# Four seams of a four-layer kernel: where a table is built, rows are returned, and a scan is opened

## The chip, the cores and the metric

One Trainium2 chip, one of its cores, one launch. The time is device microseconds of that core (us below); a kernel is timed in several runs and the median is given. The engines named here are PE (TensorE matmul; PEld is its weight load), DVE (VectorE), ACT (ScalarE), POOL (GpSimd) and SP (SyncE, which only issues transfers).

## The reference

Two images of 128 channels and 56 x 56 pixels go through four layers, each added onto x after a group norm: agent attention, a 3 x 3 convolution, a mixture of experts on 2 x 2 patches, and a selective scan in two directions along each row. The change touches the last two:

```python
# layer 2: 1568 patches (784 an image) of 512 numbers, 8 experts, two for each patch
logits = xp @ router_w
probs = softmax(logits)
topv, topi = top_k(probs, 2);  topv = topv / topv.sum(-1, keepdims=True)
gate = (one_hot(topi, 8) * topv[..., None]).sum(1)
for e in range(8):
    val, g = split(xp @ w1[e], 2, axis=-1)
    out = out + gate[:, e:e+1] * ((val * sigmoid(g)) @ w2[e])

# layer 3, once forwards and once backwards along each row of 56 pixels
xi, z = split(x @ in_w.T, 2)
xc = silu(conv_b + sum(xp[:, k:k+L] * conv_w[:, k] for k in range(4)))
dt, B, C = split(xc @ xproj_w.T, [8, 24])
dt = softplus(dt @ dt_w.T + dt_b)
h = exp(dt * A) * h + (dt * xc) * B        # 16 states for each channel
y = (h * C).sum(states) + xc * D
out = (y * silu(z)) @ out_w.T
# both directions are fused, layer-normed and added onto x
```

## The kernel before

**Experts, the table.** `PatchExperts.route` routes the patches and lays them, sorted by image and expert, into 32 tiles of 128 slots. Patches lie in 14 groups of 112 (T), seven an image. For each group and each of the two choices, `is_slot` (112 x 128) says which slot of its tile a patch takes, and `what` (112 x 64) which tile, once times the patch's number and once times its share. Lines 1291 to 1299 multiply `is_slot` transposed by `what` and sum 28 products into the bank `inv` (128 slots x 64), from which `whom` (the patch of each slot, L1301) and `share` are copied. `is_slot` and `what` lie in `room0` and `room1`, which share buffers with the expert weights (tags w2 and w1).

**Experts, the tiles.** `run` takes tile after tile. SP reads the expert's number and issues the loads of its weights (`up_weights` 4 MB, L1331; `down_weights` 2 MB, L1336), two buffers of each. `gather` fetches the 128 patches of a tile from DRAM by `whom`, an indirect transfer that POOL issues (L1306), four buffers. `up` transposes the rows (`xr_ps`, L1354), copies them (`xs_c`, L1356) and makes two halves (c) of two parts each, 16 products to a part (`h_ps`, L1365; in float32 a product is two passes), then sigmoid on ACT (L1375) and the product on DVE (`ht`, L1377). `down` (L1385, 16 passes of 512 columns) follows one tile later; ACT scales the result and stores it in `os` (L1388, L1389). 25 tiles are always there (`fewest`); the first image's are all within the first 20 (`ahead`). The rest (three here) stand in a Switch over their number.

**The return.** `combine` brings the results back into x: for each group of 112 patches two gathers from `os` (g0, g1; L1306), an add on DVE (L1461), four transposes on PE (`y_ps`, L1464), and, one call later, `onto`: four adds onto x (L1437) and their statistics (L88). It is a generator; one `next` traces one group. `arrive` runs it and then the three stages of the group norm (aggregate; means, one small product, L104; deviations, another, L116, then Ln and Exp on ACT, L67 and L68). The first image's runs beside the tiles: three leading calls (`LEAD`) at tile 20 that issue gathers only, and from then on a call at each `spot`: after either half of `up` and after `down`. The second image's runs in the opening of layer 3, without a lead.

**Layer 3.** `mamba_pair` works on 14 blocks of 448 pixels and two ways (f, b). A way has 16 units. A unit is a decay (`dA`, ACT, two instructions, L1876), a `push` (`dBu`, POOL, L1887), a `scan` (DVE, L1906), and the product with C on DVE (L1917) or POOL (L1915; `POOLED` says which), which PE then sums (`collect`, L1928). Ahead of a way's units stand its stages: `norm`, `conv` (L1752), `silu`, `low` (L1781), `step` (L1806), `log`, `softplus` (L1841), `weigh` (L1849), `send_steps` (SP and POOL transfers, L1864). They are booked by step in `agenda`. Under `manual_schedule` each engine takes the instructions of a block in the order in which they are traced. There are two such blocks: the opening (all steps below zero, and with them the second image's return), and the units' loop, which starts with `push` of the first four units, and then, at unit n, traces the decay of n + 1, what the last step left to fetch, the push of n + 4, the scan of n, a collect, and the steps booked for n. PSUM has one bank each under the tags mm and c, and two double banks under dA.

Of the kernel before, what the change touches and what calls it, by code (L numbers as in the profile page):

```python
# [8 lines left out]
F32 = mybir.dt.float32  # L9
# [8 lines left out]
P = 128  # L18
# [3 lines left out]
BLK = 448  # L22
# [991 lines left out]
class PatchExperts:  # L1014
# [15 lines left out]
    def route(self, dram, wpool, conv):  # L1030
# [9 lines left out]
        with tc.tile_pool(name="l2_route", bufs=1) as one, tc.tile_pool(  # L1040
# [13 lines left out]
            nc.vector.tensor_reduce(four, net.ident.rearrange("p (q e) -> p e q", q=4), AX.X, ALU.add)  # L1054
            shape = [T, nt, experts]
# [194 lines left out]
            inv = ps.tile([P, 512], F32, name="inv", tag="tr")  # L1250
# [4 lines left out]
            for n, room in enumerate(rooms):  # L1255
# [27 lines left out]
                for some in (range(per), range(per, nt)):  # L1283
# [7 lines left out]
                    for t in some:  # L1291
                        nc.tensor.matmul(
                            inv[:, : 2 * TILES],
                            is_slot[:, t, :],
                            what[:, t].rearrange("t h j -> t (h j)"),
                            start=n == 0 and t == 0,
                            stop=n == 1 and t == nt - 1,
                        )

            self.whom = keep.tile([P, TILES], I32, name="whom")  # L1300
# [14 lines left out]
    def run(self, wpool, work, ps, beside):  # L1315
# [12 lines left out]

        def up_weights(j, e):
            w1 = ups[j % 2]  # L1330
            nc.sync.dma_start(w1, w1s[e].rearrange("o c q f -> (o c) q f"))  # L1331
            return w1
# [8 lines left out]
        def spot():  # L1341
            with net.tc.issue_after(traced[0]):
                next(beside, None)
# [6 lines left out]
        def up(j, w1, xr):  # L1350
# [7 lines left out]
            for c in range(2):  # L1358
                parts = []
                for part in (1, 0):  # L1360
# [11 lines left out]
                    traced[0] = mm.ins  # L1372
                    parts.append(h_ps)
                sg = work.tile([P, 4 * SLOTS], F32, name="sg", tag="sg")
# [3 lines left out]
                if self.ahead + 1 < j + c < self.fewest + c:  # L1378
                    spot()
# [14 lines left out]
        for j in range(self.fewest):  # L1394
            e = expert(j)
            w1, w2 = up_weights(j, e), down_weights(j, e)
            ht = up(j, w1, gather(j))
            if last is not None:
                down(*last)
            last = (j, ht, w2)  # L1400
            if j == self.ahead:
                for _ in range(LEAD):
                    next(beside)
            elif j > self.ahead:
                spot()
# [77 lines left out]
LEAD = 3  # L1483
# [96 lines left out]
def arrive(net, combine, b, gathered, bank, banks, pool, norms, lead=0):  # L1580
# [3 lines left out]
    for stage in net.norm_stages(b, banks, "mm", got.append):  # L1584
        fetch = stage()
        if fetch:
            fetch()
        yield
# [7 lines left out]
def mamba_pair(net, out, wts, combine, keep, norms):  # L1596
# [19 lines left out]
    with ExitStack() as ctx:  # L1616
# [17 lines left out]

        class Banks:
            def tile(self, shape, dtype, name, tag):
                return wide_bank(name)[:, :512]
# [101 lines left out]
        class Half:  # L1739
# [6 lines left out]
            def conv(self, m):  # L1746
# [12 lines left out]
                if m == 0:  # L1759
                    self.xc = work.tile([P, 2, BLK], F32, name="xc", tag=f"xc{w.d}", bufs=1 if w.d == "f" else 2)  # L1760
                return lambda: nc.scalar.activation(
                    self.xc[:, m, :], pm[:, :BLK], AF.Identity, bias=w.conv_b[:, m : m + 1]
                )
# [188 lines left out]
        for n, blk in enumerate(blocks):  # L1952
# [3 lines left out]
            if n == 0:  # L1956

                book(at + 1, blk.norm)
                book(at + 3, lambda f=f: f.conv(0))
                book(at + 4, lambda f=f: f.conv(1), tag="c")  # L1960
                book(at + 6, lambda f=f: silu(f, None))
# [11 lines left out]
                book(at + 17, lambda b=b: b.conv(0))  # L1973
                book(at + 17, lambda b=b: b.conv(1), tag="c")
                book(at + 19, lambda b=b: silu(b, None))
# [67 lines left out]
        with tc.manual_schedule(engines={E.PE, E.Activation, E.DVE, E.Pool, E.SP}):  # L2043
            nc.scalar.preload_act_table_set(EXP_LN)
            second = arrive(net, combine, 1, gathered, wide_bank, ps_of_norms, keep, norms)
            first = min(agenda)
            for step in range(first, 0):
                run(step)
                for _ in range((0, 0, 0, 2, 0, 1, 1, 0, 1, 1, 1, 1, 0, 1, 1, 1)[step - first] if step - first < 16 else 1):
                    next(second, None)  # L2050
                fetch(step + 1)
            for _ in second:
                pass
        with tc.manual_schedule(engines={E.PE, E.Activation, E.DVE, E.Pool, E.SP}):
# [5 lines left out]
            for n, (h, u) in enumerate(units):  # L2060
# [15 lines left out]
                waiting.append((h, u))  # L2076

# [126 lines left out]
```

## Time and profile before

| what | us |
|---|---|
| median of 3 runs | 3035.01 (3030.69 to 3038.34) |
| profiled execution | 3033.16 |
| its span | 3031.1 |
| attention, convolution, routing | 0 to about 1012 |
| slot table, first gathers | 1012 to 1036 |
| expert tiles, both images | 1036 to 1677 |
| opening of layer 3 up to the first scan | 1677 to 1718 |
| units' loop and end | 1718 to 3031 |

The page gives the whole span's busy shares: PE 89%, DVE 72%, ACT 61%, POOL 48%. They are averages over stages with different limits, and each stage is to be read on its own: which engine has no idle time there, and what ended the idle time of the others. In a row of the order of time, the first number is the start, the second how long the group took from first start to last end, and the bracket is the engine's idle time before it and what ended that.

### The profile page before, as it was taken

Reading aid. Unit: us, or ns where it says so; the run is one execution under the profiler, and the core shown is the slowest. Engines: PE = TensorE matmul, PEld = TensorE weight load, DVE = VectorE, ACT = ScalarE, POOL = GpSimd, SP = SyncE. Lnnn points to the kernel's source line nnn. Section 1 sums busy time; section 2 is a strip of 40 time slices with the busy share of each in tenths; the row PEclk is TensorE's granted clock in tenths of the full one; section 3 lists DMA queues with packets and bytes.
Section 4 is the critical chain, followed back from the end, with each engine's and each line's share of the span. In section 5 each row is a group of like instructions: output and inputs, shape, how many; then the busy total and the mean of one; then the engine's idle time right before and its main releaser. Section 6 shows DMA issues by size and latency. Waiting matters only on the chain. (4 is left out here: it accounts for less than half of the span.)

```text
span 3031.1 us, 39355 instructions
## 1 busy us (share of the span) xinstructions
PE 2697.4 (89%) x14924; PEld 1283.4 (42%) x14924; DVE 2184.0 (72%) x1854; ACT 1853.7 (61%) x2944; POOL 1450.5 (48%) x801
## 2 busy tenths in 40 slices
PE   7999999999998799999898778888888888888874
PEld 3333333333335688788777323333333333233321
DVE  5978998999886301010120589999999999999996
ACT  5778788778751100000001488888888888888884
POOL 3000010010322100000100589999999999999995
PEclk9999999999999799999999799899899999999987
DMA  1000000000002668788875554465555565545460
GB/s 55 1 1 1 1 1 1 1 1 1 1 1 60 263 272 318 314 310 321 303 279 206 129 125 116 114 148 130 120 118 121 117 147 127 127 116 120 115 148 22
DMA packets 157934, 369.32 MB, mean 122 GB/s; under 512 B 25156, under 2 KB 114980, under 8 KB 154132
## 3 DMA queue, kind: packets, MB, share of 16 engines
q1 hardware_dynamic: 135744, 339.30, 37.5%
q0 software_dynamic: 5520, 15.62, 1.6%
q10 hardware_dynamic: 16452, 11.61, 1.2%
q8 instruction: 122, 2.00, 0.3%
q14 instruction: 96, 0.79, 0.1%
HBM read 297.89 MB, written 17.20 MB: 104 GB/s over the span
## 5 line engine op out<-in xcount | busy, mean ns | idle before, releaser
L1887 POOL TENSOR_TENSOR dBu<-dtu,Bs 128x896 f32<-128x896 f32 x448 | 921.3, 2094 | 14.4 <-DMA dtu<-sp_u 10.5
L1906 DVE TENSOR_TENSOR_SCAN h<-dA,dBu 128x896 f32<-128x896 f32 x448 | 882.3, 2009 | 28.2 <-ACT dA L1876 24.8
L620 ACT ACTIVATE ex<-sc 128x896 f32<-128x896 f32 (+1 forms) x700 | 602.6, 918 | 124.7 <-PE sc L617 113.4
L1928 PE MATMUL y<-h,both 128*64 128x448 f32 x1792 | 468.2, 615 | 82.2 <-POOL h L1915 74.9
L627 DVE TENSOR_TENSOR ex_sum<-ex_sum,ex 128x1792 f32<-128x1792 f32 (+1 forms) x238 | 492.6, 2070 | 35.3 <-ACT ex L620 21.3
L1365 PEld LDWEIGHTS h_ps<-xs_c,w 128*128 128x128 f32 x3584 | 406.5, 193 | 28.6 <-ACT ot L1388 15.4
L1365 PE MATMUL h_ps<-xs_c,w 128*128 128x128 f32 x3584 | 409.9, 277 | 9.0 <-issue 9.0
L617 PE MATMUL sc<-q,k 32*128 32x448 f32 (+1 forms) x2800 | 403.6, 587 | 3.6 <-ACT ex L620 2.9
L1917 DVE TENSOR_TENSOR h<-h,c_ps 128x1792 f32<-128x1792 f32 (+1 forms) x168 | 326.6, 1944 | 26.9 <-ACT c_ps L1894 10.1
L635 PE MATMUL av<-ex,va 128*32 128x448 f32 (+1 forms) x2800 | 334.3, 552 | 0.1
L582 POOL TENSOR_TENSOR a_e<-a_e,a_inv 112x784 f32<-112x784 f32 x14 | 41.6, 2973 | 584.0 <-ACT ex L620 394.5
L1377 DVE TENSOR_TENSOR ht<-h_ps,sg 128x512 f32<-128x512 f32 x56 | 38.5, 691 | 391.8 <-PE h_ps L1365 339.7
L1876 ACT ACTIVATE dA<-dt,f_A 128x448 f32<-128x448 f32 x448 | 282.7, 636 | 50.7 <-DVE h L1906 39.7
L1876 ACT ACTIVATE dA<-dt,b_A 128x448 f32<-128x448 f32 x448 | 282.8, 635 | 33.1 <-DVE h L1906 24.2
L1928 PEld LDWEIGHTS y<-h,both 128*64 128x64 f32 x1792 | 118.9, 147 | 354.8 <-issue 212.6
L1306 POOL DMA_INDIRECT xr<-xd,whom x28 | 28.1, 1004 | 493.3 <-PE xr_ps L1354 449.3
L1915 POOL TENSOR_TENSOR h<-h,Cs 128x1792 f32<-128x1792 f32 (+1 forms) x70 | 252.5, 3608 | 6.9 <-PE sp_ps L1841 3.4
L617 PEld LDWEIGHTS sc<-q,k 32*128 32x128 f32 (+1 forms) x2800 | 137.7, 181 | 230.1 <-issue 132.5
L1375 ACT ACTIVATE sg<-h_ps 128x512 f32<-128x512 f32 x56 | 33.4, 597 | 310.0 <-PE h_ps L1365 309.9
L1385 PE MATMUL o_ps<-w,ht 128*128 128x512 f32 x448 | 204.4, 601 | 1.2 <-DVE ht L1377 1.2
L1388 ACT ACTIVATE ot<-o_ps,share 128x512 f32<-128x512 f32 x28 | 19.2, 687 | 255.5 <-PE o_ps L1385 255.5
L625 DVE TENSOR_TENSOR ex_sum<-ex 128x1792 f32<-128x1792 f32 x56 | 114.4, 2043 | 54.5 <-ACT ex L620 54.4
(342 smaller groups left out, 3006.7 us busy)
## 6 DMA issues: line engine op xcount, KB each, us to landing
w<-in_L_conv_w_dram SPq DMA_DIRECT2D x28, 4096.0 KB, 20.4
w<-in_L_conv_w_dram SPq DMA_DIRECT2D x28, 2048.0 KB, 10.9
Bs<-far SPq DMA_DIRECT2D x56, 896.0 KB, 7.7
Cs<-far SPq DMA_DIRECT2D x448, 112.0 KB, 2.9
dtu<-sp_u SPq DMA_DIRECT2D x108, 224.0 KB, 3.8
dt<-dt SPq DMA_DIRECT2D x108, 224.0 KB, 4.9
os<-ot ACTq DMA_DIRECT2D x28, 256.0 KB, 7.9
xd<-xt SPq DMA_DIRECT2D x14, 224.0 KB, 2.7
```

The costliest lines, as they stand in the source:

```text
L617: nc.tensor.matmul(sc[:size, j, :BLK], self.m.k[rows, at : at + size], self.q[rows, :], start=True, stop=True)
L620: nc.scalar.activation(ex[:size, 2 * g : 2 * g + 2, :], sc[:size, :, :BLK], AF.Exp, scale=scale)
L627: nc.vector.tensor_add(self.total[g][:size], self.total[g][:size], ex[:size])
L635: nc.tensor.matmul(self.av[rows, :BLK], self.m.va[:size, i, rows], self.ex[i][:size, h, :], start=i == 0, stop=i == STEPS - 1,)
L1365: mm = nc.tensor.matmul(h_ps[:, i * SLOTS : (i + 1) * SLOTS], w1[:, q, f0 : f0 + P], xc[:, q, :], start=q == 0, stop=q == 3,)
L1385: mm = nc.tensor.matmul(o_ps, ht[:, i, :], w2[:, i, :], start=i == 0, stop=i == nj - 1)
L1876: nc.scalar.activation(self.dA[u][:, r * BLK : (r + 1) * BLK], self.dt2[:, m, r, :], AF.Exp, scale=self.w.A[:, j, 2 * m + r : 2 * m + r + 1],)
L1887: nc.gpsimd.tensor_tensor(self.dBu[u], self.dtu2[:, m], self.B[:, j, :].unsqueeze(1).to_broadcast(shape), ALU.mult)
L1906: nc.vector.tensor_tensor_scan(hf, af, bf, 0.0, ALU.mult, ALU.add)
L1915: nc.gpsimd.tensor_tensor(h4, h4, self.C[j].unsqueeze(1).to_broadcast(shape), ALU.mult)
L1917: nc.vector.tensor_tensor(h4, h4, self.c_ps[:, :BLK].unsqueeze(1).to_broadcast(shape), ALU.mult)
L1928: nc.tensor.matmul(self.y[r * H : (r + 1) * H, m, :BLK], both, self.hc[j][:, m, r, :], start=False, stop=j == PAIRS - 1)
```

## The change

Four parts:

- **Slot table by halves.** The operands of the 28 products change places: `what` is loaded, `is_slot` streams, and even and odd groups write to the lower and the upper 64 partitions of a new bank `turned`. It is copied to SBUF (`table`) and multiplied once by `fold` (two stacked identities of 64), which turns it and adds the halves: `inv` as before.
- **Tiles.** PE's work of tiles 1 to 3 is queued behind the first group of tile 0's products; SP's loads of a tile are queued behind the load of up weights of tile 0 (for tile 1) or 1 (later ones).
- **Return of the first image.** Four leading calls and five buffers instead of three and four. The later calls stand at places listed in `turns`: for tile 21 after the `down` that follows it; for tile 22 after the first, third and fourth part of `up` and after `down`; for tile 23 after the second and fourth part and twice after `down`; for tile 24 after the first two parts. At its norm's second stage ACT's table set for Exp and Ln is loaded.
- **Opening of layer 3.** Block 0's two ways apply silu when they read the convolution from its bank, with no second pass. Five of the second image's seven groups are returned in the opening (one after `conv`, one after `low`, one after each of the next three stages), into the dA banks; the other two, the last `onto` and the norm's stages follow in the units' loop, one call a unit right after the scan, into the bank mm.

```diff
@@ route
+            fold = one.tile([P, 2 * TILES], F32, name="fold")
+            nc.vector.tensor_add(fold, net.ident[:, : P // 2], net.ident[:, P // 2 :])
...
-            inv = ps.tile([P, 512], F32, name="inv", tag="tr")
+            turned = ps.tile([P, 512], F32, name="turned", tag="tr")
...
                     for t in some:
+                        g = t % 2 * 2 * TILES
                         nc.tensor.matmul(
-                            inv[:, : 2 * TILES],
+                            turned[g : g + 2 * TILES, :SLOTS],
+                            what[:, t].rearrange("t h j -> t (h j)"),
                             is_slot[:, t, :],
-                            what[:, t].rearrange("t h j -> t (h j)"),
-                            start=n == 0 and t == 0,
-                            stop=n == 1 and t == nt - 1,
+                            start=n == 0 and t < 2,
+                            stop=n == 1 and t >= nt - 2,
                         )
+            table = one.tile([P, SLOTS], F32, name="table")
+            nc.vector.tensor_copy(table, turned[:, :SLOTS])
+            inv = ps.tile([P, 512], F32, name="inv", tag="tr")
+            nc.tensor.matmul(inv[:, : 2 * TILES], table, fold, start=True, stop=True)
@@ run
+        starts, fetches = [], []
...
-        def spot():
-            with net.tc.issue_after(traced[0]):
-                next(beside, None)
+        turns = {1: (4,), 2: (0, 2, 3, 4), 3: (1, 3, 4, 4), 4: (0, 1)}
+
+        def spot(j, at):
+            if j < self.fewest:
+                for _ in range(turns.get(j - self.ahead, ()).count(at)):
+                    with net.tc.issue_after(traced[0]):
+                        next(beside)
...
                     traced[0] = mm.ins
+                    starts.append(mm.ins)
                     parts.append(h_ps)
+                    spot(j, 2 * c + 1 - part)
...
-                if self.ahead + 1 < j + c < self.fewest + c:
-                    spot()
...
-            e = expert(j)
-            w1, w2 = up_weights(j, e), down_weights(j, e)
-            ht = up(j, w1, gather(j))
+            behind = ExitStack()
+            if 0 < j < 4:
+                behind.enter_context(net.tc.issue_after(starts[0]))
+            if j > 0:
+                behind.enter_context(net.tc.issue_after(fetches[min(j - 1, 1)]))
+            with behind:
+                e = expert(j)
+                w1, w2 = up_weights(j, e), down_weights(j, e)
+                ht = up(j, w1, gather(j))
...
-            elif j > self.ahead:
-                spot()
+            spot(j, 4)
@@
-LEAD = 3
+LEAD = 4
@@ arrive
         fetch = stage()
+        if n == 1 and lead:
+            nc.scalar.preload_act_table_set(EXP_LN)
@@ mamba_pair
+        opening = True
+
+        def back_bank(name):
+            return wide_bank(name) if opening else mm(name)
...
-            def conv(self, m):
+            def conv(self, m, as_=AF.Identity):
...
-                return lambda: nc.scalar.activation(
-                    self.xc[:, m, :], pm[:, :BLK], AF.Identity, bias=w.conv_b[:, m : m + 1]
-                )
+                return lambda: nc.scalar.activation(self.xc[:, m, :], pm[:, :BLK], as_, bias=w.conv_b[:, m : m + 1])
...
-                book(at + 3, lambda f=f: f.conv(0))
-                book(at + 4, lambda f=f: f.conv(1), tag="c")
-                book(at + 6, lambda f=f: silu(f, None))
+                book(at + 3, lambda f=f: f.conv(0, AF.Silu))
+                book(at + 4, lambda f=f: f.conv(1, AF.Silu), tag="c")
+                book(at + 6, lambda: silu(None, None))
...
-            nc.scalar.preload_act_table_set(EXP_LN)
-            second = arrive(net, combine, 1, gathered, wide_bank, ps_of_norms, keep, norms)
+            second = arrive(net, combine, 1, gathered, back_bank, ps_of_norms, keep, norms)
             first = min(agenda)
             for step in range(first, 0):
                 run(step)
-                for _ in range((0, 0, 0, 2, 0, 1, 1, 0, 1, 1, 1, 1, 0, 1, 1, 1)[step - first] if step - first < 16 else 1):
-                    next(second, None)
+                if step - first in (3, 6, 8, 9, 10):
+                    next(second)
                 fetch(step + 1)
-            for _ in second:
-                pass
+            opening = False
...
                 waiting.append((h, u))
+                next(second, None)
```

Way b's convolution and silu change in the same manner as way f's.

## What the change should do to the time

> **What bounds the kernel now.** I read the page first, then stretches of the span one by one, then the order of time at each seam. Times are us from the span's start. The table by stretch has busy time of PE, PEld, DVE, ACT, POOL (with counts), PE's granted clock, DMA share, GB/s.
>
> ```profile
> span 3031.1 us, 39355 instructions
> 1012.00:1024.00 12.00, 12.00 (x56) 11.81 (x56) 3.70 (x7) 0.00 (x0) 0.00 (x0) 0.50 0.76 304
> 1036.00:1494.00 458.00, 458.00 (x3151) 374.91 (x3151) 42.71 (x62) 40.71 (x64) 19.95 (x20) 1.00 0.80 311
> 1494.00:1516.00 22.00, 12.84 (x75) 9.83 (x74) 5.16 (x11) 0.60 (x1) 11.88 (x12) 0.77 0.88 305
> 1593.00:1602.00 9.00, 0.00 (x0) 0.01 (x1) 1.40 (x6) 2.37 (x4) 0.00 (x0) 0.70 1.04 360
> 1717.70:1751.00 33.30, 25.28 (x59) 8.05 (x57) 21.27 (x14) 24.62 (x42) 31.93 (x15) 0.79 0.47 108
> 1800.00:2950.00 1150.00, 976.43 (x3272) 370.46 (x3272) 1112.39 (x631) 975.84 (x1753) 1120.91 (x532) 0.92 0.54 126
> ```
>
> The experts (1036 to 1677) are PE alone: 458 of 458 us busy; a PE wait there is lost one for one. The scan stage (from 1717.7) is DVE and POOL together, both 97% busy after 1800; whatever delays its first scans delays the end. The change works at four seams: the slot table, the return at 1494, the branch at 1593, the opening of the scan stage.
>
> The order of time at the first three seams, PE's rows and one of DVE:
>
> ```profile
> 1011.82 12.18 PE L1292 MATMUL inv<-room 112*128 112x64 f32 x56 [4.54 <-DVE tile_f L1267]
> 1032.05 4.36 PE L1354 MATMUL xr_ps<-ident,xr 128*128 128x128 f32 x16 [8.05 <-DMA xr<-xd,whom]
> 1036.20 14.80 PE L1365 MATMUL h_ps<-xs_c,w 128*128 128x128 f32 x128
> 1510.15 1.02 PE L1464 MATMUL y_ps<-ident,g 112*128 112x112 f32 x4 [9.16 <-DVE g L1461]
> 1510.97 8.07 PE L1385 MATMUL o_ps<-w,ht 128*128 128x512 f32 x14
> 1601.23 0.69 DVE L1356 COPY xs_c<-xr_ps 128x512 f32<-128x512 f32 x1 [5.76 <-issue]
> 1602.02 2.26 PE L1365 MATMUL h_ps<-xs_c,w 128*128 128x128 f32 x9 [9.03 <-issue]
> ```
>
> See the 9.16 us in which PE waits for the return's first rows, the same 14 matmuls that take 6.17 us elsewhere taking 8.07 at a fallen clock, and 9.03 us before the branch's first product.
>
> **Slot table and first tile.** Today 56 passes (28 products) load 128 columns and stream 64: 12.18/56 = 0.2175 us each at clock 0.50. After, they load 64 columns and stream 128 into alternate halves. Halves side by side are seen at L1928: 16 passes of 448 columns in 3.23 us, 0.20 each, where full-width 448-column passes (L1752) take 6.35/16 = 0.40. So I price a pair of passes at 0.2175: 28 pairs, 6.1 us, in two bursts of 3.05. The second burst's operands are ready on DVE at 1015.7 whatever PE does, so it ends at 1018.8. Added: a 128x128 copy 0.3 (L1180: 0.28), one product by fold 0.45 (L1176), handovers 0.25: 1019.8 instead of 1024.04, gain 4.2. Bounds: halves one after the other, -1.0; 4.2 at best, as DVE sets the second burst. The new tensor_add of fold, 0.3, is early on a DVE that waits. *By the Trainium skill, "TensorEngine Tiling (Array Packing)", Key Properties, a change of tiling mode drains the array, which speaks against half-width passes ahead of a full-width one; no row here prices it alone.* The gathers keep their 7.4 us to landing, as weights fill the DMA either way.
>
> Keeping tiles 1 to 3 behind tile 0's first group lets tile 0's product start 1.09 (4.36/4) + 0.69 + 0.2 = 2.0 after its rows land instead of 4.2: gain 2.2. The twelve transposes come back later at 0.43 a tile, 1.3, and the cold clock now falls on the products (about 3 us at half speed, 1.5 instead of 0.35): 1.2. Together **3.9**; range -1.3 to 5. Tile 0's weights land at 1027.0, before 1029.8. The SP order of weight loads is already the one asked for: nothing.
>
> **The return.** From tile 21's first product (1486.46) to the end of the group before the branch (1592.99) is 106.5 us. Four tiles of 21.81 (1464.65 to 1486.46) are 87.2, the return's own seven groups and two small products 4.9: 14.4 lost (9.16 idle, some 2 at low clock behind it, the rest where DVE waits for later rows, 11.33 us before 1542.31, and holds the bank that tile 23's transposes want). After, the first group stands behind down(20): up(21) ends at 1501.0, 16 passes of 0.428, one transposition 0.43: 1508.3. The rows are added by 1510.1: 1.8 remains. With five buffers and later calls the last rows are fetched some 15 us ahead of use. On POOL ten gathers now stand ahead of tile 25's rows (12.9 us of issue), which are wanted only at 1591. Gain **12.6**; bounds 4 (most of the wait and the later stall stay) to 14.4.
>
> **The branch.** PE's idle 9.03 ends with DVE's copy, 5.76 after DVE's last norm instruction (1595.47). Now the norm ends within tile 24, and PE's own entry counts: as long as DVE's (1592.99 + 5.76, saving 3.2) or as SP's, whose issues are 7.5 apart there (saving 1.5). I take **2.3**, bounds 0 to 3.3. The early table preload costs one more load, 1.28 us on ACT, in a tile where ACT waits over 8 us for PE; without that cover it would cost itself.
>
> **The opening.** PE, then POOL, then DVE:
>
> ```profile
> 1686.94 0.71 PE L1464 MATMUL y_ps<-ident,g 112*128 112x112 f32 x4 [2.86 <-issue]
> 1692.51 3.21 PE L1781 MATMUL low_ps<-xc,f_xp_t 128*40 128x448 f32 x4
> 1715.09 2.07 POOL L1887 TENSOR_TENSOR dBu<-dtu,Bs 128x896 f32<-128x896 f32 x1 [1.25 <-issue]
> 1719.07 10.20 POOL L1887 TENSOR_TENSOR dBu<-dtu,Bs 128x896 f32<-128x896 f32 x5 [1.91 <-DMA dtu<-sp_u]
> 1729.23 3.97 POOL L1915 TENSOR_TENSOR h<-h,Cs 128x1792 f32<-128x1792 f32 x1
> 1717.74 2.01 DVE L1906 TENSOR_TENSOR_SCAN h<-dA,dBu 128x896 f32<-128x896 f32 x1
> 1721.18 2.02 DVE L1906 TENSOR_TENSOR_SCAN h<-dA,dBu 128x896 f32<-128x896 f32 x1 [1.43 <-POOL dBu L1887]
> 1726.62 2.02 DVE L1906 TENSOR_TENSOR_SCAN h<-dA,dBu 128x896 f32<-128x896 f32 x1 [3.42 <-ACT dA L1876]
> 1748.77 2.02 DVE L1917 TENSOR_TENSOR h<-h,c_ps 128x1792 f32<-128x1792 f32 x1 [5.09 <-ACT c_ps L1894]
> ```
>
> Front: silu from the bank saves a table load (1.28) and a pass (0.95) and ends 2.3 us sooner (1684.75 for 1687.03), and low stands behind one return group, not three: 1687.65 instead of 1692.51. As many groups as before follow up to the softplus, so the first scan comes 4.9 earlier. If ACT runs way b's silus and table loads ahead of the first decay, 3 of it is lost. I take 4.9.
>
> Against it: rows 5 and 6 now stand inside the scan loop. POOL's rows follow program order (the product at 1754.97 waits 3.40 us). So gathers for row 5 are queued behind dBu 0 to 4, and DVE's add for them ahead of scan 1. From the end of dBu 0: 1.91 (dtu), four dBu 8.16, gather issues 0.30 + 0.99 + 0.30, landing 3.4 (quiet rows), add 0.69, row 4 onto x 1.47: scan 1 at 17.2, now at 4.0 (1721.18 - 1717.16). Loss 13.2. Then scan 1 (2.02), POOL's product 3.97, the gathers for row 6 4.99, add and onto 2.16: scan 2 after 13.1, now 5.44. Loss 7.7. Then the single mm bank: way b's low waits for row 5's bank, row 6 for low's, scan 3 for row 6's onto: 3.21 + 0.53 + 1.0 + 1.44 = 6.2 instead of 2.41, loss 3.8. The norm's means wait for the bank under dt_ps, and its Ln/Exp round trip holds DVE: 3.0 and 2.4, estimates from such handovers in these rows. Sum 30.1. Given back: 4.9 at the front, perhaps 2 of the 5.09 at 1748.77. **Net loss 23**; bounds 9 (the two gather waits less 5.4 in front, all of the 5.09 and 1.8 of landing) to 29 (front gain 2, nothing given back). *The Trainium skill, "DMA: Bandwidth & Descriptors", Anatomy of one DMA, gives a gather of 229 KB about 2.5 us where these rows show 3.4; by it the loss would be 1.8 smaller.* If the gathers had cover, the moved 7 us of DVE work would fit into the 12 us that DVE idles before 1751, and the loss would vanish.
>
> **Sum.** -3.9 - 12.6 - 2.3 + 23 = +4.2 on the profiled execution's 3033.16 (span 3031.1 and 2.1 around it): 3037.4. The median shown is 3035.01, 1.9 above that execution, so I predict 3039: no change that can be told, leaning slow.
>
> **Rivals.**
> 1. *The return's rows do not hold DVE in the scan loop* (the gathers get ahead of dBu, or land early): for it, DVE has 12 us of idle there and the two opening blocks are merged on ACT (decay 0 runs before way b's copies); against it, POOL's order in the loop is strict in every row. Then -18.8 - 4.9, moved work hidden: 3011. Faster.
> 2. *The return still stalls PE* (slower): at the group behind down(20), with ten gathers in the queue instead of eight and tile 22's weights landing at 1508.9; from a landing after 1514 each us costs one, and clock with it. Price: the gain there is 4, not 12.6: 3048. For it, landing took 14.0 us there; against it, later gathers took 3.4.
> 3. *The halves run one after the other*: table gain gone, 5.2 dearer: 3044.
>
> **How the numbers follow.** "Same" means within 0.3% of 3035 (3026 to 3044), about what can be told. Forecast 0.50 (own range 3029 to 3050: 0.32 same, 0.18 slower), rival 1 0.22 (faster), rival 2 0.24 (slower), rival 3 0.04 (half each). Faster 0.22, same 0.34, slower 0.44. The range takes 9 to 29 for the opening and the low return bound: 3011 to 3057.
>
> **What would show it.** Right: the cast of whom near 1020; no PE wait over 3 us at the first return group; the first scan about 24 us sooner in the span but scan 1 some 15 us behind it, DVE's wait put down to the gather; a second gap of 8 us before scan 2. Wrong: scans 0 to 3 within 12 us (rival 1), PE idle over 6 us at the return (rival 2), or the table still 12 us (rival 3).

## The result, and the profile after

| | median us | runs |
|---|---|---|
| before | 3032.58 | 15, 3029.65 to 3038.34 |
| after | 3041.57 | 15, 3036.82 to 3047.95 |
| ratio | 1.003 | 95% interval 1.0022 to 1.0039 |

The change costs 9 us, and the interval leaves out 1. The profiled execution of the changed kernel took 3047.95, the highest of its 15, so its trace shows more loss (15 us of span) than the medians do. Seam by seam I read the traces, and sums I take from the ratios. One thousandth is 3.03 us, and an interval reaches 3 to 7 us to each side, so a difference of two ratios below some 5 us is only an indication.

The table by stretch of the changed kernel, columns as in the prediction's first fence:

```profile
core 0 of [0], span 3046.1 us
1010.80:1020.00 9.20, 7.19 (x58) 6.23 (x58) 4.52 (x11) 0.00 (x0) 0.35 (x1) 0.50 0.91 367
1494.00:1528.00 34.00, 25.97 (x137) 19.46 (x137) 7.30 (x14) 1.28 (x2) 14.23 (x14) 0.80 1.05 383
1591.00:1600.00 9.00, 8.66 (x70) 7.90 (x71) 0.69 (x1) 1.14 (x2) 0.00 (x0) 1.00 0.92 308
1700.15:1762.94 62.79, 25.01 (x62) 8.49 (x62) 27.62 (x38) 22.57 (x42) 36.84 (x19) 0.67 0.33 76
```

The four seams, in turn. The table now keeps PE 7.19 us busy. At the return PE still loses 8 of 34 us. At the branch it is busy for 8.66 of 9 us, where before it had no work in 9 us. From scan 0 to scan 8 the loop takes 62.79 us for what took 32.97, and VectorE idles in 35 of them.

The order of time of PE at the first three seams:

```profile
1010.86 3.25 PE L1295 MATMUL turned<-room 112*64 112x128 f32 x28 [4.55 <-DVE tile_f L1269]
1014.80 3.25 PE L1295 MATMUL turned<-room 112*64 112x128 f32 x28 [0.68 <-DVE room L1282]
1018.45 0.69 PE L1306 MATMUL inv<-fold,table 128*128 128x64 f32 x2 [0.39 <-DVE table L1304]
1032.18 1.09 PE L1368 MATMUL xr_ps<-ident,xr 128*128 128x128 f32 x4 [13.05 <-DMA xr<-xd,whom]
1034.11 16.98 PE L1379 MATMUL h_ps<-xs_c,w 128*128 128x128 f32 x128 [0.84 <-DVE xs_c L1370]
...
1512.15 0.73 PE L1483 MATMUL y_ps<-ident,g 112*128 112x112 f32 x4 [3.32 <-DVE g L1480]
1521.81 6.43 PE L1379 MATMUL h_ps<-xs_c,w 128*128 128x128 f32 x32 [3.77 <-issue]
...
1591.30 0.63 PE L1368 MATMUL xr_ps<-ident,xr 128*128 128x128 f32 x4 [0.48 <-issue]
1592.82 14.53 PE L1379 MATMUL h_ps<-xs_c,w 128*128 128x128 f32 x128
```

Two bursts of 3.25 stand for the 12.18 of the old table. The cast of `whom` starts at 1019.17, where it was 1024.04. But the rows of tile 0 come no sooner: PE waits 13.05 for them where it waited 8.05, and starts on them at 1032.18 (1032.05 before). The return has two waits, 3.32 and then 3.77, instead of one of 9.16. At the branch the wait of 9.03 is gone.

VectorE in the opening of layer 3 (L1930 are the scans 0 to 3):

```profile
1700.15 2.02 DVE L1930 TENSOR_TENSOR_SCAN h<-dA,dBu 128x896 f32<-128x896 f32 x1 [5.02 <-POOL dBu L1911]
1716.00 0.69 DVE L1480 TENSOR_TENSOR g<-g,g 112x512 f32<-112x512 f32 x1 [13.83 <-DMA g<-os,at_i]
1718.00 2.01 DVE L1930 TENSOR_TENSOR_SCAN h<-dA,dBu 128x896 f32<-128x896 f32 x1
1729.45 0.69 DVE L1480 TENSOR_TENSOR g<-g,g 112x512 f32<-112x512 f32 x1 [9.45 <-DMA g<-os,at_i]
1731.45 2.00 DVE L1930 TENSOR_TENSOR_SCAN h<-dA,dBu 128x896 f32<-128x896 f32 x1
1735.87 0.82 DVE L1456 TENSOR_TENSOR x<-x,y_ps 128x112 f32<-128x112 f32 x4 [2.41 <-PE y_ps L1483]
1737.26 2.01 DVE L1930 TENSOR_TENSOR_SCAN h<-dA,dBu 128x896 f32<-128x896 f32 x1
...
1746.43 0.16 DVE L107 COPY gn_mean<-gn_ps 128x1 f32<-128x1 f32 x1 [3.40 <-PE gn_ps L104]
...
1760.99 2.02 DVE L1941 TENSOR_TENSOR h<-h,c_ps 128x1792 f32<-128x1792 f32 x1 [4.79 <-ACT c_ps L1918]
```

and POOL, which issues those gathers:

```profile
1702.85 8.15 POOL L1911 TENSOR_TENSOR dBu<-dtu,Bs 128x896 f32<-128x896 f32 x4 [2.73 <-DMA dtu<-sp_u]
1711.15 1.07 POOL L1313 DMA_INDIRECT g<-os,at_i  x1 [0.16 <-issue]
...
1720.09 3.95 POOL L1939 TENSOR_TENSOR h<-h,Cs 128x1792 f32<-128x1792 f32 x1 [4.44 <-DVE h L1930]
1724.19 1.02 POOL L1313 DMA_INDIRECT g<-os,at_i  x1 [0.15 <-issue]
```

The first wait of 13.83 is the predicted queue: POOL gets to the gathers of row 5 only behind four dBu (8.15), VectorE has the add for them ahead of scan 1. Then both wait for each other in turn: POOL's product at 1720.09 waits 4.44 for scan 1, and the second pair of gathers stands behind that product. The two later waits, 2.41 and 3.40, are the bank and the norm.

### The profile page after: what moved, and what is told of

The parts are those of the page before. It is cut to its first block, busy times and chain, and to the rows that moved or that the text cites. A ratio compares the mean times of both kernels' runs of the same rounds, so it can differ in the third digit from the quotient of the medians.

```text
span 3046.1 us, 39362 instructions
## 1 busy us (share of the span) xinstructions
PE 2687.5 (88%) x14926; PEld 1274.1 (42%) x14926; DVE 2183.3 (72%) x1856; ACT 1850.8 (61%) x2941; POOL 1451.0 (48%) x801
## 5 line engine op out<-in xcount | busy, mean ns | idle before, releaser
L1930 DVE TENSOR_TENSOR_SCAN h<-dA,dBu 128x896 f32<-128x896 f32 x448 | 882.5, 2009 | 30.7 <-ACT dA L1900 23.0
L1939 POOL TENSOR_TENSOR h<-h,Cs 128x1792 f32<-128x1792 f32 (+1 forms) x70 | 252.5, 3607 | 24.5 <-DVE h L1930 15.5
```

Of the source, the lines that this page charges most:

```text
L1930: nc.vector.tensor_tensor_scan(hf, af, bf, 0.0, ALU.mult, ALU.add)
L1939: nc.gpsimd.tensor_tensor(h4, h4, self.C[j].unsqueeze(1).to_broadcast(shape), ALU.mult)
```

## Experiments

Twelve kernels, each timed with runs of the kernel before on the same chip. All are edits of the changed kernel; several build on the first one.

| kernel | median us | ratio to before, 95% interval |
|---|---|---|
| open_before | 3016.92 | 0.9954, 0.9939 to 0.9969 |
| old_return | 3032.33 | 0.9997, 0.9985 to 1.0009 |
| late_call | 3030.74 | 0.9989, 0.9979 to 0.9999 |
| rows_ahead | 3029.02 | 0.9987, 0.9978 to 0.9997 |
| norm_later | 3023.26 | 0.9965, 0.9954 to 0.9977 |
| all_opening | 3024.46 | 0.997, 0.9957 to 0.9982 |
| silu_only | 3018.73 | 0.9951, 0.9932 to 0.9971 |
| w1_2k | 3034.26 | 1.0003, 0.9993 to 1.0013 |
| adds_behind | 3012.35 | 0.992, 0.9897 to 0.9943 |
| best | 3006.59 | 0.9912, 0.9893 to 0.9932 |
| best2 | 3003.45 | 0.9899, 0.9883 to 0.9916 |
| best2_old_head | 3011.24 | 0.993, 0.9913 to 0.9946 |

### The parts of the change: open_before, old_return, late_call

**open_before** undoes the opening alone: silu in its own pass, the second image's rows and norm all in the opening and in the dA banks.

```diff
-                book(at + 3, lambda f=f: f.conv(0, AF.Silu))
+                book(at + 3, lambda f=f: f.conv(0))
...
-                if step - first in (3, 6, 8, 9, 10):
-                    next(second)
+                for _ in range((0, 0, 0, 2, 0, 1, 1, 0, 1, 1, 1, 1, 0, 1, 1, 1)[step - first] if step - first < 16 else 1):
+                    next(second, None)
...
+            for _ in second:
+                pass
-            opening = False
...
-                next(second, None)
```

> The changed kernel with the opening of layer 3 as it was (silu as a second pass, all seven groups of the second image and its norm ahead of the scan loop). Theory (the opening costs about 24 us, the experts gain 10 to 12): 3019 to 3024 us, scan 1 again 4 us after the end of dBu 0, DVE never waiting for a gather inside the loop. Rival (the table and the tiles are what costs, the opening is neutral): 3038 to 3044 us.

It measured 3016.92, below the range expected: the new opening costs 0.0076 of the time, 23 us, and without it the change would have been a clear gain.

**old_return** takes back the return of the first image too, so that only the slot table and the order of the first tiles are left of the change.

```diff
-LEAD = 4
+LEAD = 3
...
-        turns = {1: (4,), 2: (0, 2, 3, 4), 3: (1, 3, 4, 4), 4: (0, 1)}
...
+                if self.ahead + 1 < j + c < self.fewest + c:
+                    spot()
...
-            spot(j, 4)
+            elif j > self.ahead:
+                spot()
```

> The changed kernel with the old opening and also the old return: three fetches ahead, one call after each tile and after each half, no spread table of turns; the slot table by halves and the order of the first tiles stay. Theory (the return's edit gave 2.0 us at the first group of transposes and 11.4 at the branch, because calls no longer end against it): 13 us more than 3016.9, 3028 to 3032, with the gap of TensorE at the branch (before: up of the first tile behind it 16.87 instead of 14.5, and 9 us idle ahead of it) back. Rival (the branch gap went for another reason, say the order of the first tiles shifting the weight loads against the branch): 3017 to 3022, no gap in the trace.

13.0 us by the ratios (0.0043), as expected: that is the return and the branch together. The gap is back, in PE's order of time:

```profile
1512.78 1.02 PE L1481 MATMUL y_ps<-ident,g 112*128 112x112 f32 x4 [9.60 <-DVE g L1478]
1603.35 16.04 PE L1375 MATMUL h_ps<-xs_c,w 128*128 128x128 f32 x128 [9.89 <-issue]
```

And what is left of the change here, the table and the order of the first tiles, is worth nothing that can be told: 0.9997.

**late_call** splits the 13 us. Only the last two calls of the return, the norm's two small products, move from between tile 24's halves to the tile's end.

```diff
-        turns = {1: (4,), 2: (0, 2, 3, 4), 3: (1, 3, 4, 4), 4: (0, 1)}
+        turns = {1: (4,), 2: (0, 2, 3, 4), 3: (1, 3, 4, 4), 4: (4, 4)}
```

> The changed kernel with the old opening, and of the return only the last two calls moved: the two products of the first image's norm (gn_ps) come after the tile that stands ahead of the branch instead of between its halves. Theory (the gap at the branch was VectorE's norm ending against the branch, so that its entry of some 6 us and the copy of the next tile's tokens come late; TensorE's own entry shows none): a gap of 6 to 10 us ahead of up of tile 25 is back and its up takes 1.5 to 2 longer, 3024 to 3029 against 3016.9 and 3018.7 measured without it. Rival (the gap went because the whole return runs earlier, or because of the gathers' lead): no gap, 3016 to 3019.

10.6 us (0.0035), more than expected; so the branch is worth 10.6 and the return's own stall 2.4, which is below what can be told from ratios. The traces agree with both: from the start of the table's products to the last `ot` of the experts it is 665.2 us before, 666.1 in old_return, 663.9 in late_call and 651.8 in open_before (one execution each; 651.4 to 655.0 in the six kernels whose table, tiles and return are those of the change). But the mechanism that I gave holds only in part. PE in its order of time:

```profile
1589.94 0.35 PE L116 MATMUL gn_ps<-gn_q,group 128*128 128x1 f32 x2 [0.79 <-DVE gn_q L110]
1598.81 1.08 PE L1368 MATMUL xr_ps<-ident,xr 128*128 128x128 f32 x4 [8.52 <-issue]
1601.40 15.50 PE L1379 MATMUL h_ps<-xs_c,w 128*128 128x128 f32 x128
```

Here PE itself comes late: 8.52 us pass between its last product and its first one behind the branch, a transposition that needs nothing of VectorE's late norm. In old_return and in the kernel before, that transposition came at most 0.52 after the last product, and PE waited behind it, for VectorE's copy. In late_call the last product ahead of the branch had itself waited for VectorE (gn_q). In the others some 6 us of `down` products stood in PE's queue behind its last such wait. One reading is that PE has an entry of its own, 8.52 here, which products queued ahead of the branch cover. It is not shown, and it does not fit in full: some 6 us of products would leave over 2 of the 8.52 to be seen, and at most 0.52 is. The price of ending the norm against the branch is shown; what PE does in those microseconds is not in the trace.

### The opening: rows_ahead, norm_later, all_opening, silu_only

**rows_ahead** issues the gathers of rows 5 and 6 together with those of row 4, in the opening; the adds and all that follows stay in the loop.

```diff
-            if k + lead < blocks:
-                come.append(fetched(k + lead))
+            for i in (k + lead,) if lead or k < 4 else (4, 5, 6) if k == 4 else ():
+                if i < blocks:
+                    come.append(fetched(i))
```

> The changed kernel with only the four gathers for rows 5 and 6 issued in the opening's last call, ahead of dBu 0; their adds, transposes and adds onto x stay in the loop. Theory (the gathers' place behind dBu 0 to 4 and behind POOL's product is most of the loss): DVE's waits of 13.8 and 9.5 us for gathers go, scan 1 comes 5 to 8 us after the end of dBu 0, 3024 to 3032 us; the waits that the single mm bank makes (2.4, 3.4 us) stay. Rival (the single bank alone holds the loop): 3038 us or more.

13 us of the 23 come back (1.003 to 0.9987). Both gather waits are gone. What remains is read from the stretch from scan 0 to scan 8, first in this kernel, then in open_before:

```profile
1705.62:1751.08 45.46, 29.35 (x63) 9.86 (x62) 30.52 (x39) 21.98 (x40) 33.43 (x15) 0.66 0.34 83
```

```profile
1703.32:1735.04 31.72, 20.20 (x56) 6.47 (x54) 20.93 (x13) 23.58 (x40) 30.44 (x14) 0.95 0.44 104
```

13.74 us more, of which VectorE's busy time is 9.59 (30.52 less 20.93) and its idle time 4.15 (14.94 less 10.79). Against this stands a front that is 2.9 sooner (scan 0 comes 38.8 after the experts' end, 41.7 in open_before). The moved work did not go into VectorE's idle time; it came on top of it. But not all of the 9.59 is work. From the same stretch of rows_ahead, a row of POOL and two of VectorE:

```profile
1728.82 4.12 POOL L1912 TENSOR_TENSOR dBu<-dtu,Bs 128x896 f32<-128x896 f32 x2
1729.54 1.39 DVE L109 TENSOR_TENSOR gn_d<-gn_mv,gn_mean 128x1 f32<-128x1 f32 x1
1730.96 2.00 DVE L110 SCALAR_TENSOR_TENSOR gn_q<-gn_d,gn_mv 128x1 f32<-128x1 f32 x1
```

These two instructions of the norm work on one column. In the changed kernel they take 0.16 and 0.22; here they take 3.0 us more, and each ends with one of POOL's two dBu (1730.9 and 1732.9). So some 6.6 of the 13.74 are moved work, 3.0 these two, and the rest idle time.

**norm_later** is rows_ahead with the norm's stages begun at unit 6 of the loop, not at unit 3.

```diff
-                next(second, None)
+                if n < 3 or n >= 6:
+                    next(second, None)
```

> The changed kernel with the gathers of the last two rows issued ahead (3029.02), and the second image's norm begun at the seventh unit of the scan loop instead of the fourth. Theory (of the 12 us that this kernel still loses against the old opening, 7 to 10 are VectorE's own work on two rows and the norm, now in the loop, and 4 are waits, among them 3.64 for the norm's first product): the wait for gn_ps falls where units already wait for c_ps, 3 to 5 us less, 3024 to 3026. Rival (the norm's round trips cost the loop the same wherever they stand): 3028 to 3030.

6.7 us less than rows_ahead (0.9965 against 0.9987): the theory's side, a little beyond its range. VectorE's wait for gn_ps is 1.40 in its trace instead of 3.64, behind a product that waits for c_ps in any case, and L109 and L110, with POOL idle beside them, take 0.16 and 0.22 again. So some of the remaining loss was the norm's round trips at a bad place.

**all_opening** goes the other way: all of the return in the opening, with the silu from the bank kept.

```diff
-                if step - first in (3, 6, 8, 9, 10):
+                if step - first in (3, 6, 8, 9, 10, 12, 13, 14, 15, 16, 17):
...
+            for _ in second:
+                pass
...
-                next(second, None)
```

> The changed kernel with all seven groups and the norm of the second image in the opening, rows 5 and 6 after both softplus groups, their gathers issued early; silu from the bank stays. Theory: the first scan comes 35 to 38 us after the experts' end (34.7 in the changed kernel, 40.7 before), the loop runs as before: 3015 to 3021 us. Rival (the earlier opening is given back in the loop by ACT or PE): no faster than the kernel with the old opening.

Missed: 3024.46, slower than open_before by 5 us (0.997 against 0.9954; 7.5 by the medians), about the least that can be told. VectorE's order of time:

```profile
1690.79 0.69 DVE L1481 TENSOR_TENSOR g<-g,g 112x512 f32<-112x512 f32 x1 [5.78 <-DMA g<-os,at_i]
1714.98 2.02 DVE L1931 TENSOR_TENSOR_SCAN h<-dA,dBu 128x896 f32<-128x896 f32 x1 [2.29 <-ACT dA L1901]
```

Scan 0 comes 48.6 us after the experts' end (ACT's last `ot`, 1666.36), where open_before has 41.7. VectorE waits 5.78 for row 4's gathers, a wait that the expectation did not have although the changed kernel has it too (5.25), and rows 5 and 6 and the norm still follow ahead of scan 0. The order of the old opening, with more groups ahead of `low`, was the better of the two. How the 7 us divide over that wait and the rest was not tried.

**silu_only** keeps the old opening and takes from the new one only that the first way's evictions apply silu.

```diff
-                book(at + 3, lambda f=f: f.conv(0))
-                book(at + 4, lambda f=f: f.conv(1), tag="c")
-                book(at + 6, lambda f=f: silu(f, None))
+                book(at + 3, lambda f=f: f.conv(0, AF.Silu))
+                book(at + 4, lambda f=f: f.conv(1, AF.Silu), tag="c")
+                book(at + 6, lambda: silu(None, None))
```

> The changed kernel with the old opening, except that the first direction's two evictions from the convolution's bank apply silu themselves (the separate silu pass and its place go). Theory (the front gain of 6 us up to the first scan comes from the eviction, and does not need the rows moved): first scan 4 to 6 us sooner after the experts' end than the 41.7 of the old opening, 3011 to 3014. Rival (up to the first scan the second image's transposes and their gathers on TensorE set the pace, so an earlier silu waits at the next product): 3015 to 3019.

The theory fell: 3018.73, no gain over open_before. Scan 0 comes 40.4 us after the experts' end, not 4 to 6 sooner than in open_before; eight kernels with the old opening have 40.3 to 43.2, so no gain can be told. PE starts `low` 15.5 after the experts' end in the kernel before, in open_before and here, and 10.6 in the changed kernel: as long as three return groups stand ahead of `low` on PE, each waiting for its rows, an earlier silu waits with them. So the 6 us by which the changed kernel's first scan is sooner (34.7 after the experts' end, 40.7 before) do not come from silu alone. They came when the groups were moved out from ahead of `low` as well; the move without silu was not tried.

### The gathers: w1_2k, adds_behind, best, best2, best2_old_head

**w1_2k** is the changed kernel with a tile's up weights fetched in four transfers of 512 columns, so that a partition's row is 2 KB long instead of 8.

```diff
-            dma = nc.sync.dma_start(w1, w1s[e].rearrange("o c q f -> (o c) q f"))
+            for i in range(4):
+                part = slice(512 * i, 512 * i + 512)
+                dma = nc.sync.dma_start(w1[:, :, part], w1s[e].rearrange("o c q f -> (o c) q f")[:, :, part])
```

> The changed kernel with each load of up weights issued as four loads of 512 columns, so that a row is 2 KB instead of 8 KB, as a gathered row is. Theory (transfers in flight share the DMA engines row by row, so 2 KB rows get a fifth against 8 KB rows): the first gathers of the return land in 6 to 9 us instead of 14, tile 0's in 7 to 9 instead of 12.5, PE's wait of 3.3 us at the first return group goes, 2 to 8 us faster than the changed kernel (3034 to 3040). Rival (they wait for the bytes issued ahead of them): landing stays at 12 to 14 us and the time at 3041.

8 us less than the changed kernel by the ratios, 7.3 by the medians. The time from issue to landing, tile 0's rows first and the first return gathers second (the last number, us), in the changed kernel and then in this one:

```profile
xr<-xd,whom POOLq DMA_INDIRECT x1, 12.4
...
g<-os,at_i POOLq DMA_INDIRECT x2, 13.7
```

```profile
xr<-xd,whom POOLq DMA_INDIRECT x1, 6.3
...
g<-os,at_i POOLq DMA_INDIRECT x2, 7.1
```

Both halve. PE's first wait at the return, 3.32 in the changed kernel, is gone in w1_2k's trace; its second, 3.77 there, is 6.33 here. Why the gathers land sooner is seen in the packets of the queues while tile 0's gathers move, two us of each kernel. q1 carries the weights, q0 the gathers; the columns are packets, MB, and the share that they took of the 16 DMA engines' time. The changed kernel (1026 to 1028), then w1_2k (1024 to 1026), then the kernel before (1030 to 1032):

```profile
q1 hardware_dynamic: 31, 1.02, 118.3%
q0 software_dynamic: 29, 0.12, 14.5%
```

```profile
q0 software_dynamic: 127, 0.45, 59.8%
q1 hardware_dynamic: 162, 0.32, 43.6%
```

```profile
q0 software_dynamic: 130, 0.41, 51.9%
q1 hardware_dynamic: 186, 0.38, 50.2%
```

In the changed kernel the two queues move about as many packets, 31 and 29, but one of up weights has 33 KB (1.02 MB by 31) and one of the gathers 4: the gathers get a seventh of the time. With packets of 2 KB on q1 they get half. The third fence shows that it is the length of the rows and not the number of transfers: there q1 carries down weights, one transfer with rows of 2 KB, and the gathers get half as well. The Trainium skill, "DMA: Bandwidth & Descriptors", Queues, rings and completion order, says that each DMA engine takes turns between its queues packet by packet; the equal counts agree with it.

**adds_behind** is open_before with one more tie: what a return call adds to VectorE stands behind the copy `xs_c` of the tile in which the call is made. In the changed kernel's order VectorE had

```profile
1514.43 0.69 DVE L1480 TENSOR_TENSOR g<-g,g 112x512 f32<-112x512 f32 x1 [0.22 <-DMA g<-os,at_i]
1517.21 0.69 DVE L1480 TENSOR_TENSOR g<-g,g 112x512 f32<-112x512 f32 x1 [2.09 <-DMA g<-os,at_i]
1519.45 0.69 DVE L1480 TENSOR_TENSOR g<-g,g 112x512 f32<-112x512 f32 x1 [1.55 <-DMA g<-os,at_i]
...
1521.02 0.68 DVE L1370 COPY xs_c<-xr_ps 128x512 f32<-128x512 f32 x1
```

that is, the adds of later rows, each waiting for its gathers, ahead of the copy that the next tile's products need at 1518. The existing tie holds PE's instructions alone.

```diff
-                    with net.tc.issue_after(traced[0]):
+                    with net.tc.issue_after(traced[0]), net.tc.issue_after(copied[0]):
...
-            nc.vector.tensor_copy(xc.rearrange("c q s -> c (q s)"), tp)
+            copied[0] = nc.vector.tensor_copy(xc.rearrange("c q s -> c (q s)"), tp).ins
```

> The changed kernel with the old opening (3016.92, which is the kernel to compare with) and one more tie: each return call's VectorE work stands behind the copy of the transposed tokens (xs_c) of the tile in which it is called. Theory (the second wait of the return's first group, 4.18 us there and 3.77 in the changed kernel's profile, is VectorE's order: adds that wait for gathers stand ahead of xs_c of the next tile): the wait of h_ps of the second return tile goes, the first one (4.14, y_ps behind the first add) stays, 3011 to 3015. Rival (it is the gathers' landing itself, and the wait only moves on to the next y_ps group on TensorE): 3016 to 3019.

3012.35, within the range; open_before had 3016.92, and the two intervals overlap, so it is the trace that shows the cause. VectorE now copies behind the first add, with no later add ahead:

```profile
1510.52 0.69 DVE L1480 TENSOR_TENSOR g<-g,g 112x512 f32<-112x512 f32 x1 [24.01 <-DMA g<-os,at_i]
...
1512.48 0.69 DVE L1370 COPY xs_c<-xr_ps 128x512 f32<-128x512 f32 x1
```

and of PE's two waits at the return only the first (4.12) is left.

**best** has the old opening, that tie and w1_2k's four transfers together.

> The same tie, the old opening, and each expert's up weights loaded in four transfers of 512 columns. Theory (2 KB gathered rows wait behind 8 KB weight rows; with 2 KB weight rows they land in 6 to 7 us instead of 12 to 14): the 7.3 us that the split gave the changed kernel come off 3016.9, and the tie takes off 4 to 6 more, since in the split kernel the wait behind xs_c was 6.33: 3003 to 3008. Rival (the split's gain and the tie's are the same wait, counted twice): 3009 to 3011.

3006.59, within the range. Whether the split and the tie add up cannot be told: by the ratios the tie alone took 10 us off open_before, the split alone 8 off the changed kernel, and both together 13 off open_before, each with 3 to 7 us of interval. Of the return one wait was left, the next tile's first part of up weights; **best2** therefore issues the four transfers in the order in which the products read them.

```diff
-            for i in range(4):
+            for i in (2, 0, 3, 1):
```

> The kernel with the old opening, the tie on VectorE and the up weights in four transfers (3006.59), with the four transfers issued in the order in which the products use them (columns 1024, 0, 1536, 512 and on). Theory (the 4.79 us that are left at the return's first group are the wait for the part of the up weights that the first half-product reads, which was issued third): the wait goes, 3001 to 3005. Rival (the four parts run side by side on the 16 engines and land together, so their order decides little): 3005 to 3008, the wait stays.

3003.45, within the theory's range, 3 to 4 us below best, which is less than can be told from the ratios. PE's wait at that place in best, and then in best2:

```profile
1510.59 6.16 PE L1381 MATMUL h_ps<-xs_c,w 128*128 128x128 f32 x32 [4.79 <-DMA w<-in_L_conv_w_dram]
```

```profile
1507.23 5.44 PE L1381 MATMUL h_ps<-xs_c,w 128*128 128x128 f32 x32 [2.74 <-ACT ot L1404]
```

The wait shrinks to 2.74 and does not go. This is the fastest kernel of the study: ratio 0.9899 to before, interval 0.9883 to 0.9916.

**best2_old_head** is best2 with the slot table and the order of the first tiles as they were before the change.

> The same kernel as best2 with the old slot table and the old order of the first tiles. Theory (the table's gain of about 4 us was real and was lost because the first tile's gathers shared the engines with 8 KB weight rows; with 2 KB rows it is kept): 3 to 5 us slower than best2. Rival (what the first gather finds on the engines is set by when the first weights are fetched, not by the table): within 2 us of best2.

7.8 us slower than best2 by the medians, more than expected. In the traces the experts end 4.6 sooner in best2 (1650.60 against 1655.18), and tile 0's rows are there 5.1 sooner (1026.39 against 1031.45). Of both, 1.15 is a table that began sooner in that execution; the rest, 3.4 and 3.9, is the gain of the new table and the new order of the first tiles. What else makes up the 7.8 is not placed.

## Why the prediction was right or wrong

The time: 3039.0 predicted, 3041.57 measured, in the range, and on the slow side of what can be told from no change. By parts, in us, from differences of the ratios:

| part | predicted | measured | between |
|---|---|---|---|
| slot table, first tile | -3.9 | -0.9 | before, old_return |
| the return's stall | -12.6 | -2.4 | old_return, late_call |
| the branch | -2.3 | -10.6 | late_call, open_before |
| the opening | +23 | +23.0 | open_before, after |
| sum | +4.2 | +9.1 | |

The -0.9 and the -2.4 are within the noise of their ratios; the traces bear out the order of size. The stretch that the prediction had at 106.5, from tile 21's first product to the last group before the branch, took 104.5 (1488.29 to 1592.78), 2.0 less. At the branch 9.0 of idle time went and 2.3 of `up` of tile 25.

**The opening: right, in mechanism and size.** Scan 1 came 17.9 us after the end of dBu 0 (17.2 predicted), scan 2 13.45 after scan 1 (13.1), scan 3 5.81 after scan 2 (6.2), and the waits are put down to the gathers, as it said. A gather among quiet rows took 3.47 from issue to add (1712.53 to 1716.00), the row's 3.4 and not the 2.5 that the prediction set beside it from the page. The next pair, beside other transfers, took 3.93. The front gained 6.0 for 4.9. What was wrong in this part is a remark: that with cover for the gathers the moved work would fit into VectorE's idle time and the loss would vanish. In rows_ahead they have cover, and 10 us of loss stay. And the front's gain was given half to silu and half to the order on PE; silu alone, in silu_only, starts `low` no sooner. Of the signs, the first scan came 17.6 sooner in the span and not 24, as the experts gained less; and PE's first wait at the return was 3.32, where a sign of being right was none over 3.

**The table: the step that failed is "the gathers keep their 7.4 us to landing, as weights fill the DMA either way".** The table itself gained 3.9 (the cast at 1019.17 for 1024.04, less a start that was 0.96 earlier), 4.2 predicted; the halves do run side by side, at 0.232 a pair for 0.2175. But the loads of both first tiles moved up too: tile 0's up weights were issued at 1006.27 (1014.47 before), where the prediction expected nothing of SP's order, and tile 1's at 1018.09 (1024.03 before), when the last burst had freed their buffer. So the gathers, issued at 1019.65, now met up weights in packets of 33 KB: 12.4 to landing. The row of 7.4 that I had used belongs to gathers beside down weights with rows of 2 KB, as the third of the queue fences shows. Weights filled the DMA either way, but not in the same pieces. The cold clock cost more too: tile 0's products took 16.98 for 14.80, 2.2 where 1.2 was priced. With rows of 2 KB the gain is there: 7.8 between best2 and best2_old_head, 3.4 of it placed in the traces.

**The return: the step that failed is "the rows are added by 1510.1: 1.8 remains", with nothing behind it.** The first wait was 3.32 for 1.8, as the gathers were issued 2.0 later and landed in 13.7 to 14.0. The larger miss is a second wait of 3.77 that the prediction does not have: it moved the return's transposes on PE and took VectorE's order for granted. Rival 2 priced the gain at 4 and its place was the right one; it blamed late landing alone, and of the 7.1 idle about half was VectorE's order, as adds_behind shows.

**The branch: right place, size off by a factor of more than four.** The step that failed is "PE's own entry counts: as long as DVE's" (saving 3.2). In the changed kernel PE's gap ahead of the branch's transposition is 0.48; why it is 8.52 in late_call stays open. So all of the 9.03 went, and up of tile 25 took 14.53 for 16.87.

**Rival 1** is out: scans 0 to 3 took 37 us, not 12. **Rival 3** is out, by the two bursts. Of the 18.8 foretold for the first three seams 13.9 came, 10.6 of it at the seam that was to give 2.3: that the sum missed by only 5 us is luck there; the opening's 23 is not. Two bounds were added up wrongly, without weight for the forecast: the opening's upper one is 28.1 by its terms (30.1 less 2), not 29, and 29 with the low return gives 3054, not 3057.

The fold product was weighed against a rule of the Trainium skill ("TensorEngine Tiling (Array Packing)", Key Properties: a change of tiling mode drains the array). It took 0.69 for its two passes, where 0.45 was priced. No run here tells a drain from the clock of 0.50 at that place; either way it is 0.24.

## What to carry to other kernels

A transfer's landing time is not a constant to be taken from a row: ask which transfers will be under way at the new moment, and in rows of what length. When work is moved on one engine, write out the new order on each other engine that feeds it, POOL's gathers and VectorE's adds included; here the largest losses stood in a queue other than the one whose order the change was made for. Work put into the loop of an engine that sets the pace need not go into that engine's idle time: in rows_ahead it cost its full time, and the waits grew besides.

## What the hardware showed that I had not expected

- Two DMA queues shared the engines by packets, not by bytes: 31 packets of 33 KB against 29 of 4 KB left the gathers 14.5% of the time; with 2 KB packets on the other side they had 52 to 60%, and landed in half the time.
- PE took 8.52 us into the branch when its last product before had just waited for VectorE, and at most 0.52 showed when some 6 us of products were queued behind its last wait. What it does in that time is not shown.
- Two one-column VectorE instructions, 0.16 and 0.22 us beside an idle POOL, took 1.39 and 2.00 beside its dBu and ended when those ended.
- PE's granted clock in the stretch from scan 0 to 8 was 0.64 to 0.70 in the four kernels with two rows and the norm in the loop, and 0.78 to 0.95 in the nine with the old opening. It is not the two gather waits alone: rows_ahead, without them, has 0.66.
